# Down products of an unpacked MLP by seven products instead of eight, beside the next sequence's delta attention

## The chip, the core and the metric

The kernel runs on one core of a Trainium2 chip. The metric is the device time of one execution in microseconds, the median over several executions. Everything is in fp32. A matmul instruction of the program shows as two records in the profile, so counts of PE records are twice those of the program.

## The reference

Two sequences of 1024 tokens with 512 features go through two pre-norm layers, each an attention and an MLP, each added to a residual stream x:

```
x = x + delta_attention(layernorm(x))      # gated delta rule, 6 heads of 64, causal conv
x = x + mlp0(layernorm(x))                 # 512 -> 4096 -> 512, 4-bit weights with block scales
x = x + latent_attention(layernorm(x))     # 16 heads
x = x + mlp1(layernorm(x))                 # 512 -> 2048 -> 512, SiLU, hidden kept 2 of 4
# mlp0:
inter = gelu(x @ Wg.T) * (x @ Wu.T)
out = inter @ Wd.T
```

The 4-bit codes and scales of Wg, Wu and Wd are input. The change concerns the last line, for sequence 0.

## The kernel before, in words

The work is laid out in stages, each a pair of streams that share the engines: a "main" stream of attention steps, and a "fill" stream of MLP pieces. `weave` (L157) advances the main stream by one step, gets back the microseconds of fill that this step wants (`FILL`, 3.3, for the delta attention), and draws pieces from the fill until their own estimates (`STEP`, 3.4, for four matmuls of 512 columns, half of that for a seven's product) have used this credit up. What is left of the fill when the main stream has ended runs alone. The order that comes out is the order in which PE, DVE (VectorE), ACT (ScalarE) and POOL (GpSimd) execute: these four are scheduled by hand. The DMA issues on SP (SyncE) are ordered by the framework.

The stages, read from the trace: to about 460 us the delta attention of sequence 0 and both sequences' front ends; to about 1242 the delta attention of sequence 1 (`Delta.second`), beside MLP 0 of sequence 0 (`Unpacked`); to 1288 the rest of that MLP alone; to about 2193 the latent attention of sequence 0 beside MLP 0 of sequence 1 (`Second`); then the attention of sequence 1 beside the sparse MLP of sequence 0; at last the sparse MLP of sequence 1 (`Sevens`).

MLP 0 is cut into eight chunks of 512 hidden features. `Unpacked` expands the codes on the way: for each half of a chunk's gate, up and down weights, `Codes.values` (L917 ff.) makes two pieces of three DVE instructions (nib, L925 and L926, and a multiplication with the scales, L929), and the result is also stored to DRAM (`kept`) for sequence 1. `plan` queues these pieces as jobs, three for each part (the third forms the left sums of a gate or up part on POOL and stores it), and `core.spend(n)` executes n jobs between two pieces of MLP work. The first two chunks go by plain matmuls (`chunk`). From the third on (`rest`), gate and up go by a scheme that multiplies two 2 x 2 block matrices with seven block products instead of eight (`SEVEN`, L211):

```
    (1, 0, True, "11", "11"),
    (2, 1, True, "12", "21"),
    (6, 0, False, "S2", "T2"),
    (5, 1, True, "S1", "T1"),
    (7, 0, False, "S3", "T3"),
    (3, 1, False, "S4", "22"),
    (4, 0, False, "22", "T4"),
```

Each row names the product, which of two PSUM banks it goes to, whether it starts the bank afresh, and the left and right factor. S1 to S4 and T1 to T4 are sums of blocks (`left_sums` and `right_sums`, from L226). Products 1, 6 and 5 are copied from PSUM by ACT (`part`, L991); after 2, 7, 3 and 4 DVE adds the bank to the destination, and for 2, 7 and 3 a copied part is added one product later (`soon`, run by `step`). `macro` does a gate or up half of a chunk in seven pieces of four matmul records of 512 columns (z_ps, L1018).

The down product of `Unpacked` is plain: `outcome` (L1154 ff.) takes the eight tiles of 128 tokens, multiplies each by the chunk's down weights with four matmuls of 512 columns into one bank (o_ps, L201), adds it to the token tile x on DVE (L1161), and spends one job. In the last chunk each x tile is stored (parked) right after its addition. The down products of `Second` already go by sevens: `Seven.output` (L1056 ff.) is called for two passes over half of the tokens, q = 0 and 1, each with seven products of four matmuls of 256 columns (z_ps, L1064); left sums of h on DVE (L957), right sums of the weights on POOL (L239 to L242 when called with POOL), x additions on DVE (L1079) and, for the copied parts, on POOL (L1081).

`Delta.second` works on eight chunks of 128 tokens as three overlapping streams per slot: `early` (prepare, then solve, a triangular solve on DVE by rows, L603 and L604), `late` (invert, then advance, which updates the state S: R at L683 and L684, matmuls L689, L397, L703 and L720, Ud at L693, o at L698 and L726, S at L715) and `normed`. `fetch` loads what the front end had stored for a chunk: cv, the convolved values, and gw, the output gate.

At the handover `mlp[1].open()` loads the first gate weights of `Second` (z_left) and sums them on POOL, then the first product of `Second` can start; its first two chunks' gate and up weights are stored without sums and are loaded as four blocks.

Of the kernel before, what the change touches and what calls it, by code (L numbers as in the profile page):

```python
# [26 lines left out]
F32 = mybir.dt.float32  # L27
# [9 lines left out]
P = 128  # L37
# [25 lines left out]
class Pools:  # L63


    def __init__(self, tc):
        self.tc, self.open_ = tc, {}
# [14 lines left out]
class Core:  # L82
# [171 lines left out]
class Delta:  # L254
# [570 lines left out]
    def second(self, stored, away, fill):  # L825


        core, nc, a = self.core, self.core.nc, self.a
        self.open(1, 2)

        def fetch(c):
            d = self.d[c]
            d["cv"] = self.ring("cv", [P, 3 * NG, P], 2)
            nc.sync.dma_start(out=d["cv"], in_=self.away[c][0])
            d["gw"] = self.ring("gw", [P, NH, DH], 3)
            nc.sync.dma_start(out=d["gw"], in_=self.away[c][1])
# [36 lines left out]
        for slot in range(CH + 2):  # L873
            if slot + 1 < CH:
                fetch(slot + 1)
# [84 lines left out]
class Seven:  # L960
# [95 lines left out]
    def output(self, left, right, at, adder):  # L1056
# [17 lines left out]
        for p, ps in self.products(multiply):  # L1074
# [6 lines left out]
                    self.soon.append(lambda x=x, v=parts[{2: 1, 7: 5, 3: 6}[p]]: adder.tensor_add(x, x, v))  # L1081
            yield p

    def places(self, x, q):

        dm = DM // 2
        return [
            [x[:, 4 * m + 2 * q : 4 * m + 2 * q + 2, v * dm : (v + 1) * dm] for v in range(2)] for m in range(2)
        ]


class Unpacked(Seven):
# [3 lines left out]

    EARLY = 2

    def __init__(self, core, banks, codes, xT, kept, park):
        super().__init__(core, banks, AF.Gelu_apprx_tanh, core.nc.vector)  # L1100
        self.codes, self.xT, self.kept, self.park = codes, xT, kept, park
        self.wp = core.pools("f_h", side="right")
        self.nib = core.pools("f_nib", 2, side="right")
        self.plain = core.pools("f_w", 2, side="right")
        early = (("gate", 0), ("up", 0), ("gate", 1), ("up", 1), ("down", 0), ("down", 1))
        later = (("gate", 0), ("up", 0), ("down", 0), ("gate", 1), ("up", 1), ("down", 1))
        self.order = [(c, *part) for c in range(NC0) for part in (early if c < self.EARLY else later)]
        self.ws = {}
        self.staged = {u: codes.load(u) for u in self.order[:2]}

    def tile(self, u):

        c, w, half = u
        away = self.kept[u]
        if w == "down":
            t = self.wp.tile([P, 2, 512], F32, tag="w_down", bufs=3, name="w_down")
# [37 lines left out]
    def outcome(self, c, hs, tbs):  # L1154

        core, nc = self.core, self.core.nc
        wd = [self.ws[c, "down", half] for half in range(2)]
        for n in range(4 * tbs[0], 4 * tbs[-1] + 4):
            po = self.banks.one("o_ps")
            product(nc, po, [(h, wd[s // 2][:, s % 2, :]) for s, h in enumerate(hs(n))])  # L1160
            nc.vector.tensor_add(core.x[n], core.x[n], po)  # L1161
            if c + 1 == NC0:
                nc.sync.dma_start(out=self.park[n], in_=core.x[n])
            core.spend(3 - len(tbs))
            yield STEP

    def chunk(self, c, tb, swap=None):
# [19 lines left out]
        yield from self.outcome(  # L1187
            c, lambda n: [h[:, s, n % 4 * P : n % 4 * P + P] for s in range(4)], (tb,)
        )
        core.spend()  # L1190

    def first_tokens(self):
# [16 lines left out]
    def macro(self, c, half, w, g):  # L1209

        left = self.blocks(self.ws.pop((c, w, half)))
        for p in self.gate(left, g) if w == "gate" else self.up(left, g):
            self.step(p, 0)
            self.core.spend(1)
            yield STEP / 2
        self.core.spend()

    def rest(self):
        core = self.core
        parts = ("gate", 0), ("up", 0), ("gate", 1), ("up", 1), ("down", 0), ("down", 1)  # L1220
        self.plan(0, *parts)
        for c in range(self.EARLY):
            yield from self.chunk(c, 1, self.swap if c + 1 == self.EARLY else None)
        for c in range(self.EARLY, NC0):
            gs = [self.wp.tile([P, 2, 2, T // 2], F32, tag=f"h{half}", name="h0") for half in range(2)]
            for (half, w), ahead in zip(
                ((0, "gate"), (0, "up"), (1, "gate"), (1, "up")),
                (("down", 0), ("gate", 1), ("up", 1), ("down", 1)),
            ):
                self.plan(c, ahead)  # L1230
                yield from self.macro(c, half, w, gs[half])
            self.step(4, 0)
            self.plan(c + 1, ("gate", 0), ("up", 0))
            yield from self.outcome(
                c,
                lambda n: [gs[s // 2][:, s % 2, n // 4, n % 4 * P : n % 4 * P + P] for s in range(4)],
                (0, 1),
            )
            core.spend()
        core.pools.close("f_z", "f_nib", "f_h")  # L1240


class Second(Seven):
# [41 lines left out]
    def right_factors(self, wd):  # L1285
        half = DM // 2
        blocks = {
            f"{i + 1}{j + 1}": wd[:, 2 * i : 2 * i + 2, j * half : (j + 1) * half] for i in range(2) for j in range(2)
        }
        new = [self.wp.tile([P, 2, half], F32, name=f"wd_t{i}") for i in range(2, 5)]  # L1290
        right = right_sums(self.core.nc.gpsimd, blocks, new)
        return {name: [t[:, k, :] for k in range(2)] for name, t in right.items()}

    def left(self, hs, q, calls):

        blocks = {
            f"{i + 1}{j + 1}": hs[j][:, :, i, q * HB : (q + 1) * HB] for i in range(2) for j in range(2)
        }
        new = [self.wp.tile([P, 2, HB], F32, name=f"h_s{i}") for i in (1, 2, 4)]
        return left_sums(Recorder(self.core.nc.vector, calls), blocks, new)  # L1300

    def run(self):
        core, nc = self.core, self.core.nc
        todo, ws = self.todo, self.ws
        for c in range(NC0):
            wd = self.down_weights(c)
            hs = []
            for pair in range(2):
                g = self.wp.tile([P, 2, 2, T // 2], F32, tag=f"h{pair}", name="h0")
                hs.append(g)  # L1310
                for w in ("gate", "up"):
# [4 lines left out]
                    for p in self.gate(left, g) if w == "gate" else self.up(left, g):  # L1316
# [1 line left out]
                        if p == 3 and i < len(todo):  # L1318
                            self.sums(todo[i])
                        if p == 3 and (w, pair) == ("up", 0):  # L1320
                            right = self.right_factors(wd)
                        yield STEP / 2
            calls = deque()
            lefts = [self.left(hs, 0, calls)]
            for q in range(2):
                for p in self.output(lefts[q], right, self.places(self.x, q), nc.gpsimd):
                    self.step(p, 0)
# [2 lines left out]
                        while calls:  # L1330
                            calls.popleft()()
                    if q == 0 and p == 4:
                        lefts.append(self.left(hs, 1, calls))
# [661 lines left out]
def two_layers(ctx, tc, a):  # L1995
# [1 line left out]
    core = Core(ctx, tc)  # L1997
    pools = core.pools
    banks = Banks(ctx, tc)
    core.hold(pools("x0", side="right"), 0)  # L2000


    kept = {}
# [10 lines left out]
    mlp = []  # L2014

    def some():
        mlp.append(Unpacked(core, banks, Codes(core, pools("codes", 2, side="right"), a), xT_0, kept, parks[0]))
        return mlp[0].first_tokens()

    delta.first(xT_0, some)  # L2020
# [125 lines left out]
```

## Time and profile before

| | |
|---|---|
| median of 3 runs | 3213.23 us (3211.96 to 3216.2) |
| the profiled execution | 3214.91 us, its span 3213.2 |
| mean granted TensorE clock | 0.979 |
| PE, DVE, ACT, POOL busy | 97%, 60%, 29%, 24% |
| HBM | 70 GB/s over the span |
| chain that ended last | PE 81%, DVE 9%, POOL, issue, ACT and DMA 2% each |
| x<-x,o_ps on DVE (L1161) | 64 of 686 ns |
| x<-x,z_ps on DVE (L1079, `Second`) | 64 of 683 ns |
| x<-x,part on POOL (L1081, `Second`) | 48, mean 1460 ns |
| right sums of wd on POOL (L239 to L242) | 32, 1275 to 1490 ns |
| part<-z_ps on ACT (L991) | 288 of 586 ns |

A row of groups names line, engine, operation, output and inputs, shape and count, then busy time in us and the mean of one in ns, then the idle time of that engine just before these instructions and what ended it. PE is the busy engine almost everywhere, so a change matters by what it does to the time of PE's own instructions and to the gaps between them. PE's clock is granted by the chip; the profile states it as a share of full speed for any stretch.

### The profile page before, as it was taken

The numbers are of one execution on the slowest core, as the hardware profiler recorded it, in microseconds if no ns is written. First come the engines' busy times: TensorE is split into PE (matmuls) and PEld (weight loads), VectorE is DVE, ScalarE is ACT, GpSimd is POOL, SyncE is SP. The second block draws the span as 40 slices with busy tenths as digits, with TensorE's granted clock in tenths as the row PEclk, the third lists the DMA queues.
The fourth block names the chain that finished last, engine by engine and source line by source line (L and its number), as shares of the span: only waits on it lengthen the run. The fifth ranks groups of instructions, "written<-read, shape, count | busy, mean of one in ns | idle before, by whom it ended". The sixth has DMA issues, their size and how long they took to land.

```text
span 3213.2 us, 35654 instructions
## 1 busy us (share of the span) xinstructions
PE 3106.8 (97%) x13012; PEld 1626.1 (51%) x13012; DVE 1925.1 (60%) x3569; ACT 931.2 (29%) x1338; POOL 766.6 (24%) x822
## 2 busy tenths in 40 slices
PE   7999899999999999999999999999999999999998
PEld 6787754555555554555434444446433243224547
DVE  6888752466666554367577656745674367244766
ACT  5544311122222211311453125522113401432221
POOL 3323101122222211356321221222003600450000
PEclk9999899999999999999999999999999999999999
DMA  2111234132332224246112111142010010015211
GB/s 90 35 29 29 67 96 142 32 122 91 97 95 86 76 94 164 70 137 207 66 37 69 53 48 37 35 141 72 20 40 1 14 53 14 7 37 167 76 46 49
DMA packets 194638, 228.08 MB, mean 71 GB/s; under 512 B 53728, under 2 KB 148448, under 8 KB 194080
## 3 DMA queue, kind: packets, MB, share of 16 engines
q1 hardware_dynamic: 194464, 225.81, 22.2%
q8 instruction: 103, 1.69, 0.2%
q14 instruction: 71, 0.58, 0.1%
HBM read 153.11 MB, written 72.61 MB: 70 GB/s over the span
## 4 chain that ended last, share of the span: by engine, by line
PE 81%; DVE 9%; POOL 2%; issue 2%; ACT 2%; DMA 2%; SPq 1%; DVEq 0%; POOLq 0%; ACTq 0%
PE z_ps L1018 23%; PE o_ps L201 12%; PE z_ps L1064 8%; PE u_ps L201 5%; PE g_ps L201 5%; PE st_ps L1564 5%; PE s_ps L1506 4%; PE av_ps L1582 3%; PE proj_ps L201 2%; PE small_ps L630 1%; PE wide_ps L640 1%; DVE cv L469 1%; PE wide_ps L558 1%; DVE rd L1634 1%; PE den_ps L1603 1%
## 5 line engine op out<-in xcount | busy, mean ns | idle before, releaser
L991 ACT COPY part<-z_ps 128x512 f32<-128x512 f32 x288 | 168.7, 586 | 738.4 <-PE z_ps L1018 505.5
L1018 PE MATMUL z_ps<-xT,z_left 128*128 128x512 f32 x768 | 361.8, 601 | 3.1 <-DMA z_left<-in_w_gate 3.0
L1515 DVE TENSOR_REDUCE top<-s_ps 128x2 f32<-128x1024 f32 x256 | 301.0, 1217 | 80.4 <-PE s_ps L1506 80.3
L1574 ACT ACTIVATE es<-st_ps 128x1024 f32<-128x1024 f32 x256 | 248.3, 1021 | 175.9 <-PE st_ps L1564 171.0
L1018 PE MATMUL z_ps<-xt,z_left 128*128 128x512 f32 x576 | 274.3, 598 | 1.2 <-DVE z_h L1036 1.0
L1018 PEld LDWEIGHTS z_ps<-xT,z_left 128*128 128x128 f32 x768 | 142.0, 191 | 191.6 <-issue 164.0
L201 PE MATMUL o_ps<-w_down,h 128*128 128x512 f32 x512 | 229.6, 599 | 0.4 <-DVE part L1052 0.4
L1596 POOL TENSOR_TENSOR es<-es 128x512 f32<-128x512 f32 x128 | 159.3, 1276 | 148.7 <-ACT es L1574 78.0
L1018 PE MATMUL z_ps<-xT,w_left 128*128 128x512 f32 x384 | 181.5, 602 | 5.0 <-DVE part L1052 2.7
L1564 PE MATMUL st_ps<-q,kT 17*128 17x512 f32 x1024 | 178.3, 650 | 4.3 <-ACT es L1574 1.1
L1018 PEld LDWEIGHTS z_ps<-xt,z_left 128*128 128x128 f32 x576 | 106.2, 190 | 145.7 <-issue 123.3
L1052 DVE TENSOR_TENSOR part<-z_ps,part 128x512 f32<-128x512 f32 x108 | 74.4, 689 | 174.1 <-PE z_ps L1018 168.5
L1506 PE MATMUL s_ps<-kT,q 16*128 16x512 f32 x1024 | 156.6, 647 | 6.6 <-DVE top L1515 6.6
L201 PEld LDWEIGHTS o_ps<-w_down,h 128*128 128x128 f32 x512 | 95.2, 191 | 110.5 <-issue 106.3
L201 PE MATMUL proj_ps<-xT,wqkv 128*128 128x256 f32 x576 | 136.6, 392 | 12.2 <-ACT gw L427 12.2
L1582 PE MATMUL av_ps<-es,v 128*32 128x512 f32 x1024 | 138.9, 615 | 0.0
L1018 PE MATMUL z_ps<-xt,w_left 128*128 128x512 f32 x288 | 137.0, 598 | 0.7 <-DVE part L1052 0.7
L1053 POOL TENSOR_TENSOR h<-h,part 128x512 f32<-128x512 f32 x48 | 66.5, 1387 | 280.1 <-DVE part L1052 280.1
L1621 DVE TENSOR_TENSOR acc<-acc,es 128x1024 f32<-128x1024 f32 x96 | 131.7, 1419 | 0.0
L201 PEld LDWEIGHTS proj_ps<-xT,wqkv 128*128 128x128 f32 x576 | 109.3, 195 | 31.6 <-ACT gw L427 15.1
L1036 DVE TENSOR_TENSOR h<-z_ps,part 128x512 f32<-128x512 f32 x84 | 57.9, 690 | 102.4 <-PE z_ps L1018 89.3
L201 PE MATMUL o_ps<-sdown,h 128*128 128x512 f32 x256 | 117.1, 601 | 0.0
(311 smaller groups left out, 5164.9 us busy)
## 6 DMA issues: line engine op xcount, KB each, us to landing
sums<-factor SPq DMA_DIRECT2D x24, 512.0 KB, 3.3
kept_gate<-w_left SPq DMA_DIRECT2D x12, 896.0 KB, 3.7
kept_up<-w_left SPq DMA_DIRECT2D x12, 896.0 KB, 3.9
z_left<-kept_gate SPq DMA_DIRECT2D x12, 896.0 KB, 4.6
z_left<-kept_up SPq DMA_DIRECT2D x12, 896.0 KB, 4.6
kept_down<-w_down SPq DMA_DIRECT2D x16, 512.0 KB, 3.0
wd<-kept_down SPq DMA_DIRECT2D x16, 512.0 KB, 4.2
xl<-park SPq DMA_DIRECT2D x32, 256.0 KB, 2.7
```

Source lines behind the costliest of these rows:

```text
L201: nc.tensor.matmul(ps, lhsT, rhs, start=(i == 0), stop=(i == len(pairs) - 1))
L991: self.core.nc.scalar.copy(t, src)
L1018: self.core.nc.tensor.matmul(ps, left[l][:, k, :], self.right[r][:, k, :], start=(first and k == 0), stop=(k == 1), skip_group_check=True,)
L1052: nc.vector.tensor_add(v, ps, v)
L1064: nc.tensor.matmul(ps[:, i * dm : (i + 1) * dm], left[l][:, k, i * P : (i + 1) * P], right[r][k], start=(first and i == 0 and k == 0), sto ...
L1506: nc.tensor.matmul(tiles[h4 // 2][:, h4 % 2 * 512 : h4 % 2 * 512 + 512], q1s[t][r : r + HALF, gr, :], kT[r : r + HALF, gr, j * 512 : (j + ...
L1515: nc.vector.tensor_reduce(top[:, j, h : h + 2], tiles[e].rearrange("p (i k) -> p i k", i=2), AX.X, ALU.max, negate=True)
L1564: nc.tensor.matmul(tiles[h4 // 2][:, h4 % 2 * 512 : h4 % 2 * 512 + 512], kT[r : r + CR, gr, kt * P : (kt + 1) * P], q2[r : r + CR, gr, :], ...
L1574: nc.scalar.activation(t.rearrange("p i q -> p (i q)"), tiles[e], AF.Exp, scale=HALF**-0.5)
L1582: nc.tensor.matmul(av[gr][32 * h4 : 32 * h4 + 32, :], v[:, kt, 4 * gr + h4, :], es[u][h4 // 2][:, h4 % 2, :], start=(kt == 0), stop=(kt == ...
L1596: nc.gpsimd.tensor_add(t, t, es[u][h4 // 2][:, h4 % 2, :])
L1621: nc.vector.tensor_add(t, es[u - 1][e] if kt == 1 else t, es[u][e])
```

## The change

Chunks 2 to 7 of sequence 0's MLP 0 get their down products by sevens. `outcome` stays for chunks 0 and 1; `outputs` takes its place in `rest`. With it come these edits:

- x of sequence 0 is one tile of 128 x 8 x 512 instead of eight, so that a pass can add to two token tiles at once.
- The down weights of a chunk are one tile of 128 x 4 x 512 with one buffer, `wd`, instead of two tiles from a ring of three. Its second half is unpacked during the gate half 1, together with up half 1 (six jobs), and nothing is planned for up half 1.
- `right_factors` (POOL) is called after product 3 of up half 1. `left` queues the sums of h on DVE: three at product 1 of a pass, the fourth at product 6. S3 and S4 are written over blocks of h.
- A fill piece of the down product is 1.7 us of estimate instead of 3.4, with one job each.
- The eight stores to park come together after the last chunk's second pass.
- In `Delta.second`, cv has one buffer instead of two and is fetched after the first step of the chunk's predecessor's prepare; gw has two buffers instead of three and is fetched with x in `late`.

Instructions of the program, before and after: PE 6996 and 7140 (192 matmuls of 512 columns less, 336 of 256 more), DVE 3571 and 3619, ACT 1340 and 1376, POOL 827 and 887, SP 1416 both.

```diff
     def hold(self, pool, b):
-        for n in range(b * TT, (b + 1) * TT):
-            self.x[n] = pool.tile([P, DM], F32, tag=f"x{n}", name=f"x{n}")
+        x = pool.tile([P, TT, DM], F32, name="x")
+        for n in range(TT):
+            self.x[b * TT + n] = x[:, n, :]
+        return x
...
-            d["cv"] = self.ring("cv", [P, 3 * NG, P], 2)
+            d["cv"] = self.ring("cv", [P, 3 * NG, P], 1)
             nc.sync.dma_start(out=d["cv"], in_=self.away[c][0])
-            d["gw"] = self.ring("gw", [P, NH, DH], 3)
-            nc.sync.dma_start(out=d["gw"], in_=self.away[c][1])
...
         def early(c):
             if c < CH:
-                yield from self.prepare(c)
+                steps = self.prepare(c)
+                next(steps)
+                if c + 1 < CH:
+                    fetch(c + 1)
+                yield
+                yield from steps
...
                 nc.sync.dma_start(out=x, in_=a["x"][(CH + c) * P : (CH + c + 1) * P, :])
+                gw = self.d[c]["gw"] = self.ring("gw", [P, NH, DH], 2)
+                nc.sync.dma_start(out=gw, in_=self.away[c][1])
...
+    def left(self, hs, q, calls, pool, again=False):
+        blocks = {
+            f"{i + 1}{j + 1}": hs[j][:, :, i, q * HB : (q + 1) * HB] for i in range(2) for j in range(2)
+        }
+        names = (1, 2) if again else (1, 2, 4)
+        new = [pool.tile([P, 2, HB], F32, tag=f"h_s{i}", bufs=1, name=f"h_s{i}") for i in names]
+        if again:
+            new.append(blocks["12"])
+        return left_sums(Recorder(self.core.nc.vector, calls), blocks, new)
...
+            if half == 0:
+                self.wd = self.wp.tile([P, 4, 512], F32, tag="wd", name="wd")
+            t = self.wd[:, 2 * half : 2 * half + 2, :]
...
             self.step(p, 0)
             self.core.spend(1)
+            if p == 3 and (half, w) == (1, "up"):
+                self.factors = self.right_factors(self.wd, self.sevens)
             yield STEP / 2
...
+    def outputs(self, c, gs):
+        core, nc = self.core, self.core.nc
+        calls = deque()
+        left = self.left(gs, 0, calls, self.sevens, True)
+        for q in range(2):
+            for p in self.output(left, self.factors, self.places(self.x, q), nc.gpsimd):
+                self.step(p, 0)
+                if p == 1:
+                    while len(calls) > 1:
+                        calls.popleft()()
+                elif p == 6:
+                    calls.popleft()()
+                elif p == 4 and q == 0:
+                    left = self.left(gs, 1, calls, self.sevens, True)
+                core.spend(1)
+                yield STEP / 2
+        if c + 1 == NC0:
+            self.step(4, 0)
+            for n in range(TT):
+                nc.sync.dma_start(out=self.park[n], in_=core.x[n])
+        core.spend()
...
-                (("down", 0), ("gate", 1), ("up", 1), ("down", 1)),
+                ((("down", 0),), (("gate", 1),), (("up", 1), ("down", 1)), ()),
             ):
-                self.plan(c, ahead)
+                self.plan(c, *ahead)
                 yield from self.macro(c, half, w, gs[half])
-            self.step(4, 0)
             self.plan(c + 1, ("gate", 0), ("up", 0))
-            yield from self.outcome(
...
-            core.spend()
+            yield from self.outputs(c, gs)
```

More of the change, by code (lines that the diff above doesn't have):

```diff
@@ L873, in second @@
         for slot in range(CH + 2):
-            if slot + 1 < CH:
-                fetch(slot + 1)
             streams = [normed(slot - 2), late(slot - 1), early(slot)]
@@ L1082, in output, with right_factors @@
             yield p
+    def right_factors(self, wd, pool):
+        half = DM // 2
+        blocks = {
+            f"{i + 1}{j + 1}": wd[:, 2 * i : 2 * i + 2, j * half : (j + 1) * half] for i in range(2) for j in range(2)
+        }
+        new = [pool.tile([P, 2, half], F32, tag=f"wd_t{i}", bufs=1, name=f"wd_t{i}") for i in range(2, 5)]
+        right = right_sums(self.core.nc.gpsimd, blocks, new)
+        return {name: [t[:, k, :] for k in range(2)] for name, t in right.items()}
+    def left(self, hs, q, calls, pool, again=False):
+        blocks = {
+            f"{i + 1}{j + 1}": hs[j][:, :, i, q * HB : (q + 1) * HB] for i in range(2) for j in range(2)
+        }
+        names = (1, 2) if again else (1, 2, 4)
[3 more added lines that the diff above has]
+        return left_sums(Recorder(self.core.nc.vector, calls), blocks, new)
     def places(self, x, q):
@@ L1097, with __init__ @@
     EARLY = 2
-    def __init__(self, core, banks, codes, xT, kept, park):
+    def __init__(self, core, banks, codes, xT, x, kept, park):
         super().__init__(core, banks, AF.Gelu_apprx_tanh, core.nc.vector)
-        self.codes, self.xT, self.kept, self.park = codes, xT, kept, park
+        self.codes, self.xT, self.x, self.kept, self.park = codes, xT, x, kept, park
         self.wp = core.pools("f_h", side="right")
@@ L1114, in tile @@
         away = self.kept[u]
-        if w == "down":
-            t = self.wp.tile([P, 2, 512], F32, tag="w_down", bufs=3, name="w_down")
+        if w == "down" and c + 1 < self.EARLY:
+            t = self.plain.tile([P, 2, 512], F32, tag="w_down", name="w_down")
+        elif w == "down":
+            if half == 0:
+                self.wd = self.wp.tile([P, 4, 512], F32, tag="wd", name="wd")
+            t = self.wd[:, 2 * half : 2 * half + 2, :]
         elif c < self.EARLY:
@@ L1152, in plan, with outcome @@
                 self.core.jobs.extend([lambda p=pieces: next(p, None)] * 3)
-    def outcome(self, c, hs, tbs):
+    def outcome(self, c, h, tb):
         core, nc = self.core, self.core.nc
         wd = [self.ws[c, "down", half] for half in range(2)]
-        for n in range(4 * tbs[0], 4 * tbs[-1] + 4):
+        for n in range(4 * tb, 4 * tb + 4):
             po = self.banks.one("o_ps")
-            product(nc, po, [(h, wd[s // 2][:, s % 2, :]) for s, h in enumerate(hs(n))])
+            col = slice(n % 4 * P, n % 4 * P + P)
+            product(nc, po, [(h[:, s, col], wd[s // 2][:, s % 2, :]) for s in range(4)])
             nc.vector.tensor_add(core.x[n], core.x[n], po)
-            if c + 1 == NC0:
-                nc.sync.dma_start(out=self.park[n], in_=core.x[n])
-            core.spend(3 - len(tbs))
+            core.spend(2)
             yield STEP
@@ L1186, in chunk @@
             self.plan(c + 1, ("gate", 1), ("up", 1), ("down", 0), ("down", 1))
-        yield from self.outcome(
-            c, lambda n: [h[:, s, n % 4 * P : n % 4 * P + P] for s in range(4)], (tb,)
-        )
+        yield from self.outcome(c, h, tb)
         core.spend()
@@ L1227, in rest @@
                 ((0, "gate"), (0, "up"), (1, "gate"), (1, "up")),
-                (("down", 0), ("gate", 1), ("up", 1), ("down", 1)),
+                ((("down", 0),), (("gate", 1),), (("up", 1), ("down", 1)), ()),
             ):
-                self.plan(c, ahead)
+                self.plan(c, *ahead)
                 yield from self.macro(c, half, w, gs[half])
-            self.step(4, 0)
             self.plan(c + 1, ("gate", 0), ("up", 0))
[L1234 to L1238, printed above, removed]
-            core.spend()
+            yield from self.outputs(c, gs)
         core.pools.close("f_z", "f_nib", "f_h")
@@ L1283, in down_weights @@
         return wd
[L1285 to L1300, printed above, removed]
     def run(self):
@@ L1320, in run @@
                         if p == 3 and (w, pair) == ("up", 0):
-                            right = self.right_factors(wd)
+                            right = self.right_factors(wd, self.wp)
                         yield STEP / 2
             calls = deque()
-            lefts = [self.left(hs, 0, calls)]
+            lefts = [self.left(hs, 0, calls, self.wp)]
             for q in range(2):
@@ L1332, in run @@
                     if q == 0 and p == 4:
-                        lefts.append(self.left(hs, 1, calls))
+                        lefts.append(self.left(hs, 1, calls, self.wp))
                     if q == 1 and p == 1:
@@ L1999, in two_layers @@
     banks = Banks(ctx, tc)
-    core.hold(pools("x0", side="right"), 0)
+    x_0 = core.hold(pools("x0", side="right"), 0)
     kept = {}
@@ L2016, in some @@
     def some():
-        mlp.append(Unpacked(core, banks, Codes(core, pools("codes", 2, side="right"), a), xT_0, kept, parks[0]))
+        mlp.append(Unpacked(core, banks, Codes(core, pools("codes", 2, side="right"), a), xT_0, x_0, kept, parks[0]))
         return mlp[0].first_tokens()
```

## The prediction

> **What bounds the kernel now.** I read the page first, then the stages by windows, then the chain of waits at the end of the stage that changes, then PE's waits and the timeline.
>
> ```profile
> span 3213.2 us, 35654 instructions
> PE 3106.8 (97%) x13012; PEld 1626.1 (51%) x13012; DVE 1925.1 (60%) x3569; ACT 931.2 (29%) x1338; POOL 766.6 (24%) x822
> ...
> L201 PE MATMUL o_ps<-w_down,h 128*128 128x512 f32 x512 | 229.6, 599 | 0.4 <-DVE part L1052 0.4
> ```
>
> PE is busy for 97% of the span, and the products that the change replaces had to wait only 0.4 us in all. (A matmul of the program stands as two records.) By stage, with the columns PE, PEld, DVE, ACT, POOL busy, clock:
>
> ```profile
> 660.00:1221.00 561.00, 551.33 (x2299) 310.12 (x2298) 327.00 (x705) 123.78 (x201) 134.04 (x151) 0.99 0.30 92
> 1260.00:1290.00 30.00, 30.00 (x71) 13.28 (x70) 6.96 (x11) 0.16 (x1) 0.66 (x2) 1.00 0.29 101
> 1490.00:2115.00 625.00, 623.12 (x2731) 282.99 (x2731) 411.73 (x458) 244.12 (x305) 147.13 (x117) 0.99 0.17 57
> ```
>
> 660 to 1221 is sequence 1's delta attention beside this MLP: PE is idle for 9.7 us of 561, while DVE, at 58%, and POOL, at 24%, have room on average. 1260 to 1290 is MLP work alone. 1490 to 2115 is the next MLP, whose down products go by sevens already: DVE at 66%, yet PE idle for 2 us. The chain at the handover to that MLP:
>
> ```profile
> 1253.44 7.13 PE z_ps L1018 x16
> 1260.58 27.47 PE o_ps L201 x64
> 1288.04 10.30 PE z_ps L1018 x24
> ```
>
> The last chunk's down products take 27.47 us, and `Second`'s first product follows without a wait. A seventh product, late in the next stage, beside a busy DVE:
>
> ```profile
> 2179.75 1.89 PE L1064 MATMUL z_ps<-wd,h 128*128 128x256 f32 x8
> ...
> 2181.91 1.89 PE L1064 MATMUL z_ps<-wd,h 128*128 128x256 f32 x8
> 2183.64 1.89 PE L1064 MATMUL z_ps<-wd_t,h_s 128*128 128x256 f32 x8
> 2186.23 1.99 PE L1064 MATMUL z_ps<-wd,h_s 128*128 128x256 f32 x8 [0.26 <-DVE x L1079]
> ```
>
> Eight records of 256 columns start 1.73 us after the last eight (2181.91 to 2183.64): 0.215 us each, as x64 in 27.47 is 0.429 for 512. And one place where PE waits:
>
> ```profile
> 1191.24 1.16 PE L397 MATMUL wide_ps<-S,qkT 64*128 64x64 f32 x12
> 1193.73 2.56 PE L689 MATMUL small_ps<-R,X 128*128 128x64 f32 x12 [1.33 <-DVE R L684]
> 1196.22 2.03 PE L397 MATMUL wide_ps<-S,qkT 64*128 64x64 f32 x12
> 1198.18 4.99 PE L201 MATMUL o_ps<-w_down,h 128*128 128x512 f32 x8
> ```
>
> Twelve L397 take 1.16 us before the wait of 1.33 and 2.03 after it; eight L201 take 4.99, not 3.43. The granted clock is 0.66 from 1193 to 1203.
>
> **Products: -20.6 us.** A chunk's down product is 32 matmuls, 64 records, 27.47 us. By sevens it is 2 passes x 7 products x 4 matmuls = 112 records of 0.2145 = 24.0. 3.43 saved, times six chunks. The weave gives the delta steps 3.3 us of fill each as before, so the time comes off the end of the stage, where the MLP runs alone. There are 112 weight loads for 64, at 190 ns. The Trainium skill ("TensorE: Matmul & The Clock Gate", Back-to-back issue gap) says that the spacing of load-and-matmul pairs is set by both; if they added, a chunk would cost 112 x (0.190 + 0.2145) = 45 us, six of them +106. The 1.73 us above has just such pairs, and decides: loads are hidden.
>
> **Finer fill: -4.6.** The 1.33 us wait arises where a delta step gets no piece of fill, because a piece is 3.4 us against a credit of 3.3. In the changed order 1.7 us pieces stand there. The wait goes, and the 3.3 us that the slow clock costs (0.34 of 10 us). Next there is DVE's R chain itself, 1.2 us, under 1.7 of fill.
>
> **DVE in the first of a chunk's two passes: +13.4.** What is added is cheap on average: per chunk 8 sums of h at 0.69 and 8 x adds of 0.68 for 8 old ones of 0.69. But the four unpack pieces of the next chunk (0.42 + 0.43 + 0.69 = 1.54 each) now fall in the first four products, and a bank must be drained in one product of 1.72 us where it had 3.44. In 17.8 us of PE, DVE has adds 2.7, s1 to s4 2.7, unpack 6.2, the last up product 1.4, and its delta share of about 3.7, 6 or more where the solve rows fall there. The order on DVE is fixed, so I set the two orders side by side. Chunk 2: PE from the end of product 2 to product 4 has, from the same lines' rows, L689 about 1.4, L397 1.1, products 6 and 5 3.44, L703 1.1, L720 1.3, products 7 and 3 3.44: 11.8. DVE has to be through with what remains of s1 to s3 1.5, an unpack piece 1.54, add 0.68, unpack 1.54, Ud and o 1.1, solve rows 7 to 10 2.3, s4 0.69, unpack 1.54, S twice 1.42, o 0.56, rows 11 to 13 2.6, and only then product 7's add 0.68: 16.2. Product 4, which reuses the bank, is 4.4 late; three later lags bring about 7.0. Chunk 5, counted in the same way (s4 2.5 late, product 7's add 3.3, then 0.6): 6.4. Chunks 3, 4, 6 and 7 have no solve rows there: 0 to 0.5 each, 1.5 together. Bounds for all: 5 (if DVE enters these passes ahead) to 22.
>
> **Clock after these gaps: +4** (0 to 10). After 1.33 us of wait the clock fell; after 0.9 us (three waits near 822, 899 and 1253) it did not; after 3.68 us near 645 it was 0.58 for 8 us. The skill's clock gate part (same page, Part 1) has the clock fall only after an idle window of about 3.4 us. By that rule only one gap here is long enough; by the 1.33 us row each of about three costs 3.3. I take a little over one.
>
> **POOL and ACT: 0.** POOL gets 4 right sums at 1.27 and 6 x adds at 1.3 to 1.5 per chunk, 13 to 14 us on an engine that is idle for three quarters of the stage. The right sums are issued after product 3 of the last up quarter; product 6 is the first to need a late one, T2, the third (3.8 us), and three products (5.2) and delta steps stand before it. The delta chain over POOL (AT, the block inverse) has about 5 us. Uncovered, each would cost at most its 1.3 us. ACT's 6 copies of 0.586 replace nothing and add 3.5 us per chunk on an engine at 22%. A rule that speaks against the change is in "SBUF — State Buffer", Who interferes with whom: a DVE instruction with two SBUF inputs and a POOL instruction that reads SBUF lock each other out for an instruction's length. The h sums have a median of 0.69 and a maximum of 1.75, the nib operations 0.42 and 2.02, which fits. If each of 10 POOL operations per chunk delayed DVE by half its length, it would be 6.5 us of DVE per chunk; but the next stage has the same ten and PE idle for 2 us in 625, so I take nothing, and leave the lock to the slow rival.
>
> **Memory, one tile of x, cv and gw: 0.** SP has as many issues. `cv` with one buffer is fetched after prepare's first step, when its transposes are done, and needed a slot later; `gw` comes with `x`, more than 10 us ahead of its use. Bounds 0 and 3 if a fetch landed late once.
>
> **Handover: +7** (3 to 9). Before, the loads of z_left for `Second` were issued at 1249 and its kept_up at 1255, ahead of the parks; the parks were spread over eight L201 tiles. Now eight parks wait on the last adds, on DVE and then POOL, in one block, and stand on SP ahead of the z_left loads. SP issues in order, 0.33 us each. From the last product: POOL's add about 0.4 after, four parks behind it 1.3, and the load lands 2.7 later: 4.3 of PE idle. The page's median landing for z_left is 4.6, which gives 6. The clock: after a 3.02 us wait for z_left at 2906 it was 0.50 to 2910 and 0.89 to 2914, 2.3 us; after 3.68 us it cost 3.3. 4.3 + 2.7.
>
> **Sum.** -20.6 - 4.6 + 7.0 + 6.4 + 1.5 + 4 + 7 = +0.7 on the profiled execution's 3214.91 us (span 3213.2, 1.7 around it), which lies 1.7 over the median, 3213.23. So about 3214. 0.2%, what a measurement of this kernel can tell from no change, is 6.4 us.
>
> **The rivals.** *The gain arrives*: DVE keeps up, as it does in the next stage, where PE idles 0.26 us beside a saturated DVE. Against it: no unpack is in that stage. -20.6 - 4.6, handover +4 to +7, stalls 0 to 8, clock 0 to 3: 3192 to 3206, middle 3200. 0.31. *The gain is eaten*, as summed: 3207 to 3220. 0.35. *DVE's lateness takes over in every chunk* (the slower side): the first pass has 17.8 us of PE and about 16.7 of DVE in chunks 3, 4 and 6; from 1.1 us of lock-out by POOL per pass on, each gap passes 1.3 us and takes the clock along. Then three more gaps of 1.5 and 3.3, +14, and the full 3.3 in chunks 2 and 5, +2.6: 3231, 3220 to 3238. For it: the nib maximum of 2.02. Against it: the average loads. 0.34. *The change doesn't do what it says*: if loads paced the 256-column matmuls there would be no saving; the 1.73 us row excludes it.
>
> **How the numbers follow.** The eaten gain is the likeliest by a little, so its sum is the point, 3214; almost all of it lies within 0.2%. The gain case reaches from 3192 to 3206 with its middle at 3200, and about a third of its 0.31 lies under 3197; about a third of the slow case's 0.34 lies over 3230. That leaves out 0.1 on each side.
>
> **What would show it.** L1064-like products with starts 1.72 apart (first step); no PE wait for R near 1193 (second); PE waits for DVE's x adds in chunks 2 and 5, 4 and 3 us long, with PEclk dips behind (third, fourth); at the end a PE wait for the DMA into z_left of 4 to 6 us and slow first products (last). It is wrong if PE's waits for x adds stay under 3 us in all, if `Second` starts without a wait, or if the delta steps wait for POOL or for `cv`.

## The result and the profile after

The changed kernel took 3222.53 us (median of 8, 3216.96 to 3226.29) against 3212.3 (8 runs, 3206.05 to 3216.2): ratio 1.0033, interval 1.0022 to 1.0044. It is slower by 10 us. The profiled execution has a span of 3220.9 us. From its page, in the order of the lines shown of before:

```profile
span 3220.9 us, 36455 instructions
...
PE 3092.0 (96%) x13300; PEld 1683.7 (52%) x13300; DVE 1991.8 (62%) x3617; ACT 950.9 (30%) x1374; POOL 859.0 (27%) x882
```

PE has 15 us less to do, in a span that is 8 us longer. DVE has 67 us more, where 48 more instructions of 0.69 make 33. The same columns by window, 660 to 1221 as before, and the handover:

```profile
660.00:1221.00 561.00, 534.70 (x2496) 350.45 (x2494) 387.60 (x748) 140.54 (x231) 211.03 (x201) 0.99 0.31 95
...
1294.00:1300.00 6.00, 0.60 (x2) 0.43 (x2) 0.69 (x1) 0.00 (x0) 0.61 (x1) 0.82 0.73 236
1300.00:1308.00 8.00, 8.00 (x14) 3.28 (x14) 1.63 (x4) 1.03 (x2) 4.31 (x10) 0.71 0.89 279
```

PE's idle time in the first stretch goes from 9.7 to 26.3 us. PE's waits from 600 to 1300, the head of the list (total us, times, longest):

```profile
PE z_ps L1070 <- DVE x L1085: 8.1, 5, 3.8
PE z_ps L1024 <- DMA z_left<-kept_gate: 5.4, 1, 5.4
PE small_ps L705 <- DVE Ud L695: 4.6, 2, 3.7
PE z_ps L1070 <- DVE h L963: 3.8, 1, 3.8
...
PE small_ps L632 <- DMA T<-dT: 2.0, 2, 1.7
PE small_ps L151 <- DVE ln_xn L143: 1.1, 1, 1.1
```

The first, second and fourth are new, and so are the two at the end; Ud had 3.7 us in one wait before. The chain at the handover, which answers to the three lines shown of before (start, length, what):

```profile
1292.59 0.70 DVE x L1085
...
1293.35 1.27 POOL x L1087
...
1296.48 0.55 SPq L1320
...
1297.07 2.55 DMA z_left<-kept_gate
1299.62 10.47 PE z_ps L1024 x18
```

DVE's last add, POOL's add, the parks on SP, then the load: 7 us during which PE does nothing but end its last product.

Chunk 2's passes, PE first and then DVE at the same time:

```profile
738.22 0.94 PE L705 MATMUL small_ps<-Ud,kn 128*128 128x128 f32 x6 [0.94 <-DVE Ud L695]
738.99 1.45 PE L722 MATMUL small_ps<-U,pT 128*128 128x64 f32 x12
740.27 1.95 PE L1070 MATMUL z_ps<-wd_t,h 128*128 128x256 f32 x8
742.10 1.97 PE L1070 MATMUL z_ps<-wd,h 128*128 128x256 f32 x8
747.85 3.30 PE L1070 MATMUL z_ps<-wd_t,h 128*128 128x256 f32 x8 [3.78 <-DVE x L1085]
750.94 2.30 PE L1070 MATMUL z_ps<-wd,h 128*128 128x256 f32 x8
754.31 1.99 PE L1070 MATMUL z_ps<-wd,h 128*128 128x256 f32 x8 [1.07 <-DVE x L1085]
```

```profile
743.45 0.71 DVE L717 TENSOR_TENSOR S<-S,small_ps 64x192 f32<-64x192 f32 x2
744.19 0.56 DVE L728 TENSOR_TENSOR o<-o,small_ps 128x384 f32<-128x384 f32 x1
...
746.58 0.32 DVE L606 TENSOR_REDUCE inv<-prod 48x13 f32<-48x169 f32 x1
747.01 0.69 DVE L1085 TENSOR_TENSOR x<-x,z_ps 128x512 f32<-128x512 f32 x1
747.62 0.42 DVE L931 TENSOR_SCALAR nib<-codes 128x512 int32<-128x512 int32 x1
748.07 1.37 DVE L932 TENSOR_SCALAR nib<-nib 128x512 int32<-128x512 int32 x1
```

Product 7 (740.27) has long been done when DVE, after S, o and the solve rows, comes to its add at 747.01. The product that needs the bank starts 3.78 us late, as its record at 747.85 says, and takes 3.30 us instead of 1.95: the slow clock. A nib instruction beside POOL's add (747.84 to 749.15) takes 1.37 us, not 0.43.

For everything below I use the length of the stage, from the first z_ps<-w_left product to the first z_ps<-z_left product. The part before it has the same instructions in the same order on PE, DVE, ACT and POOL in these kernels, and still it ends between 642.5 and 654.4 us in their profiles, so whole spans of single profiles mislead by some 10 us. A stage is read from one profile too: plain_down below has the products of before and a stage 2.8 us shorter, so I make nothing of differences of 3 us between two stages. The stage of before and of after (columns as above):

```profile
642.50:1287.90 645.40, 629.60 (x2489) 346.54 (x2489) 375.20 (x798) 135.62 (x222) 150.63 (x175) 0.99 0.33 103
```

```profile
647.40:1299.60 652.20, 615.60 (x2776) 400.55 (x2776) 444.49 (x847) 156.11 (x258) 239.71 (x229) 0.99 0.32 100
```

The stage is 6.8 us longer: PE busy 14.0 less, PE idle 20.8 more (15.8 to 36.6).

### The profile page after: what moved, and what is told of

It is laid out like the page before. It is cut to its first block, busy times and chain, and to the rows that moved or that the text cites. A ratio compares the mean times of both kernels' runs of the same rounds, so it can differ in the third digit from the quotient of the medians.

```text
span 3220.9 us, 36455 instructions
## 1 busy us (share of the span) xinstructions
PE 3092.0 (96%) x13300; PEld 1683.7 (52%) x13300; DVE 1991.8 (62%) x3617; ACT 950.9 (30%) x1374; POOL 859.0 (27%) x882
## 4 chain that ended last, share of the span: by engine, by line
PE 79%; DVE 11%; POOL 3%; issue 2%; ACT 2%; DMA 1%; SPq 1%; DVEq 0%; POOLq 0%; ACTq 0%
PE z_ps L1024 24%; PE z_ps L1070 11%; PE o_ps L203 7%; PE u_ps L203 5%; PE g_ps L203 5%; PE st_ps L1596 5%; PE s_ps L1538 4%; PE av_ps L1614 3%; PE proj_ps L203 2%; DVE cv L471 1%; PE small_ps L632 1%; PE wide_ps L642 1%; DVE prod L605 1%; PE wide_ps L560 1%; PE den_ps L1635 1%
## 5 line engine op out<-in xcount | busy, mean ns | idle before, releaser
L997 ACT COPY part<-z_ps 128x512 f32<-128x512 f32 x324 | 189.5, 585 | 852.1 <-PE z_ps L1024 494.4
L1087 POOL TENSOR_TENSOR x<-x,part 128x512 f32<-128x512 f32 x84 | 117.9, 1405 | 277.7 <-DVE x L1085 263.9
L1070 PE MATMUL z_ps<-wd,h 128*128 128x256 f32 x544 | 130.1, 388 | 6.2 <-DVE h L963 3.8
L1085 DVE TENSOR_TENSOR x<-x,z_ps 128x512 f32<-128x512 f32 x112 | 75.9, 682 | 78.9 <-PE z_ps L1070 75.9
```

What stands on the lines that cost most here:

```text
L997: self.core.nc.scalar.copy(t, src)
L1070: nc.tensor.matmul(ps[:, i * dm : (i + 1) * dm], left[l][:, k, i * P : (i + 1) * P], right[r][k], start=(first and i == 0 and k == 0), sto ...
```

## The experiments

Ratios are against the kernel before, timed beside each. Stage, idle and busy are PE's in the stage of one profile, in us.

| kernel | ratio | interval | stage | idle | busy |
|---|---|---|---|---|---|
| before | 1 | | 645.4 | 15.8 | 629.6 |
| changed | 1.0033 | 1.0022 to 1.0044 | 652.2 | 36.6 | 615.6 |
| plain_down | 0.9997 | 0.9986 to 1.0007 | 642.6 | 13.4 | 629.2 |
| before_half_pieces | 0.9987 | 0.9976 to 0.9997 | 641.3 | 14.4 | 626.9 |
| z_early | 1.0024 | 1.0014 to 1.0034 | 646.9 | 29.2 | 617.7 |
| spread | 1.0027 | 1.0017 to 1.0036 | 649.0 | 34.2 | 614.8 |
| both | 1.0017 | 1.0009 to 1.0026 | 646.4 | 28.8 | 617.6 |
| all_loads | 0.9995 | 0.9987 to 1.0002 | 643.6 | 27.8 | 615.8 |
| no_pool_adds | 0.9999 | 0.9990 to 1.0009 | 643.2 | 29.9 | 613.3 |
| direct_adds | 1.0034 | 1.0021 to 1.0047 | 651.7 | 31.9 | 619.8 |
| no_h_sums | 0.9979 | 0.9970 to 0.9988 | 637.9 | 27.1 | 610.8 |
| moved_unpack | 0.9998 | 0.9989 to 1.0006 | 644.2 | 30.4 | 613.8 |
| sevens_3_6_7 | 0.9989 | 0.9978 to 0.9999 | 638.3 | 19.9 | 618.4 |
| sevens_3_4_6_7 | 1.0004 | 0.9992 to 1.0016 | 647.5 | 25.8 | 621.7 |

**plain_down**: memory and loads of the change, plain products.

```diff
-            yield from self.outputs(c, gs)
+            yield from self.flat(c, gs)   # outcome of before, on the one tile wd
```

> The changed kernel with its memory and loads (x of the sequence in one tile, wd with one buffer, cv with one and gw with two, fetched later, second half of the down weights unpacked earlier), but with the plain down products of before in 128x512 matmuls and parks tile by tile. Theory (the arrangement of memory and loads costs nothing): within 3 us of the kernel before, 3209 to 3216. Rival (cv or gw, fetched later, hold up PE at the starts of slots): 4 us or more above the kernel before.

0.9997. The arrangement of x, wd, cv and gw is free, as predicted; the stage is no longer than before.

**before_half_pieces**: the kernel before with finer fill.

```diff
-            product(nc, po, [(h, wd[s // 2][:, s % 2, :]) for s, h in enumerate(hs(n))])
+            for s, (l, r) in enumerate(pairs):
+                nc.tensor.matmul(po, l, r, start=s == 0, stop=s == 3)
+                if s == 1 and len(tbs) == 2:
+                    yield STEP / 2
...
-            yield STEP
+            yield STEP / len(tbs)
```

> The kernel before, with the plain down product of chunks 1 to 7 handed out in pieces of two matmuls (1.7 us) instead of four. Theory (part of the change's worth is its finer fill: no delta step without fill at 1193, the wait of 1.33 us and the slow clock behind it go): 3 to 5 us less than the kernel before. Rival (another delta step waits in its place): within 2 us.

0.9987, 4.2 us, with an interval that stays just under 1, and 4.1 in the stage. From 1185 to 1205 PE has no idle time and a clock of 1.00. This part of the change's worth can be had without the sevens.

**z_early**: z_left in a pool of its own, its first load ahead of the parks.

```diff
+    def ahead(self):
+        self.lp = self.core.pools("g_l")
+        self.todo = [(c, w, half) for c in range(NC0) for half in range(2) for w in ("gate", "up")]
+        self.ws = {self.todo[0]: self.weights(self.todo[0])}
...
             mlp.append(Second(core, banks, xT, x, kept, parks[0]))
+            mlp[1].ahead()
```

> The changed kernel, with the buffers for the next MLP's gate and up weights in a pool of their own that is opened earlier, so that the first weights are loaded ahead of the parks. Theory (the handover costs a wait for the load of z_left, 5.4 us, and the slow clock behind it, 2 to 3): 7 to 9 us less than the changed kernel, 3213 to 3216, no wait of PE for z_left near 1295. Rival (the load only moves, and the next thing, the left sums on POOL or the first x tile of the attention, is as late): less than 2 us gained.

1.0024, some 3 us less, which the two intervals do not separate: neither theory as it stood. The wait for z_left is gone, and the stage is 5.3 us shorter, but 14 us later there is another. DVE and then PE of this run:

```profile
1310.58 0.69 DVE L128 BATCH_NORM_STATS2 ln_st<-xl 128x6 f32<-128x512 f32 x1 [4.74 <-DMA xl<-park]
...
1311.61 1.29 DVE L1042 TENSOR_TENSOR h<-z_ps,part 128x512 f32<-128x512 f32 x2
```

```profile
1312.35 3.78 PE L1024 MATMUL z_ps<-xt,z_left 128*128 128x512 f32 x4 [3.70 <-DVE h L1042]
```

DVE stands for 4.74 us at the attention's second x tile, whose load is issued on SP behind wd, wlat, wqu, wkvu and rope; the MLP's adds are queued behind it, and PE waits 3.70. The changed kernel has no such wait, as PE was late there itself.

**all_loads**: z_early and spread, and the first wd load later.

```diff
-            wd = self.down_weights(c)
+            wd = self.down_weights(c) if c else None
...
+                        if p == 4 and wd is None:
+                            wd = self.down_weights(c)
```

> Early load of the next MLP's first weights and spread unpacking as before, and the load of its first down weights moved behind its first gate half, so that the attention's second x tile is loaded ahead of them. Theory (at the handover the wait for z_left was only replaced by DVE waiting for that x tile, 3.7 to 4.0 us of PE): no wait above 1 us from 1285 to 1320 but the one for POOL near 1340 that both kernels have, 4 to 6 us less than the run with both edits, about 3213 to 3215. Rival (x tiles are late for another reason, the memory that they reuse): the wait stays above 3 us.

0.9995, against 1.0017 for both: 0.22%, 7 us, and no wait of PE over 0.25 us from 1285 to 1330. The profiles show the 7 us where they should be: the fiftieth record of a z_left product starts 36.0 us after the first in both, and 29.3 after it here, as in before. In the changed kernel it is 32.0: 2.7 later, by the slow clock. With the wait of 5.40 the handover there costs 8.1 us.

**spread** and **both**: the unpack jobs spread over both passes; both adds z_early.

```diff
-                core.spend(1)
+                if (p in (2, 5, 3)) if q == 0 else (p in (1, 6, 7, 4)):
+                    core.spend(1)
```

> The changed kernel, with the six jobs that unpack the next chunk's first weights spread over all fourteen products of the two passes (every second one) instead of the first six. Theory (DVE is late in the first pass because four unpack pieces of 1.54 us lie among its adds): PE's waits for x adds and h sums in chunks 2 to 7, 16 us in the changed kernel's profile, fall to 4 to 8, and some slow clock goes with them: 8 to 14 us less, 3208 to 3214. Rival (it is the sums of h, the solve rows or a lock by POOL that make DVE late, not the unpacking): less than 4 us gained, and the waits in chunks 2 and 5 stay at about 5 us each.

> Both of the two edits together: early load of the next MLP's weights, and unpacking spread over both passes. Theory (two separate costs of a change that is a gain by itself): they add up, 16 to 22 us less than the changed kernel, 3200 to 3206, which is 0.2 to 0.4% under the kernel before. Rival (the gain of the products is lost at a third place too): not under 3209.

1.0027 and 1.0017: the rivals were right. Spreading takes 2 us off, within the intervals; the waits for DVE became 2.96 at product 4 of chunk 2 (3.78 before) and 1.63 and 2.56 in chunk 5 (3.83, 1.04, 1.01), with a new one of 2.41 for R at 755. Both together come to 5 us and stay 0.17% above the kernel before.

**no_pool_adds**: `self.soon = []` ahead of `self.step` in `outputs`, so that POOL's additions to x are left out.

> The changed kernel without POOL's 36 additions of copied parts to x (they are left out, so sequence 0's MLP 0 misses those terms). DVE's list of instructions is the same. Theory A (POOL's instructions lock DVE's two-input and nib instructions out, which is where the remaining waits come from): DVE's mean nib instruction (second one, 599 ns in the changed kernel, 463 with plain down products) and the h sums (863 to 1005 ns) come down most of the way, PE's waits in the stage fall by 6 us or more, 6 to 10 us less than the changed kernel, about 3213 to 3217. Theory B (DVE is late by the number and order of its own instructions): waits and time as in the changed kernel within 3 us.

0.9999, 11 us under the changed kernel: a little more than theory A had. The second nib instruction of DVE, from 640 to 1300 (count, busy us, mean ns), with plain down products, in the changed kernel, and here:

```profile
L932 DVE TENSOR_SCALAR nib<-nib 128x512 int32<-128x512 int32 x71 | 32.8, 463 | 2.4
```

```profile
L932 DVE TENSOR_SCALAR nib<-nib 128x512 int32<-128x512 int32 x72 | 43.1, 599 | 2.5
```

```profile
L932 DVE TENSOR_SCALAR nib<-nib 128x512 int32<-128x512 int32 x72 | 34.7, 481 | 2.5
```

So POOL's adds do stretch DVE's instructions, by 8.4 us over 72 of these, and the 48 sums of h by 5.4 (44.8 to 39.4). PE's idle time falls by 6.7 us, as theory A asked, but not mainly in the passes: the waits in chunks 2 and 5 are still 3.78 and 1.49, 2.90 and 1.32. The handover's wait is 2.72 us, not 5.40, without POOL's last add, and a wait of 2.14 for h, 13 us later, takes most of that back. PE's other waits in the stage fall by 4.0 us and its busy time by 2.3. A part of that is chance: after the same wait of 3.78 us the clock fell in the changed kernel and did not fall here (last section):

```profile
745.05 1.97 PE L1070 MATMUL z_ps<-wd_t,h 128*128 128x256 f32 x8 [3.78 <-DVE x L1085]
```

**direct_adds**: DVE adds those products from PSUM.

```diff
+            if p in (1, 6, 5) and adder is None:
+                x = {1: at[0][0], 6: at[0][1], 5: at[1][1]}[p]
+                nc.vector.tensor_add(x, x, ps.rearrange("p (i d) -> p i d", i=2))
```

> The changed kernel, in which DVE adds products 1, 6 and 5 from PSUM to x directly, in place of ACT's 36 copies and POOL's 36 additions: 36 instructions of 0.68 us more on DVE, none of them with two SBUF inputs. Theory A (lock by POOL): DVE's busy time in the stage rises by 24 for the adds and falls by 15 to 25 for the stretched ones, the time falls or stays, -5 to 0 us against the changed kernel. Theory B (count of DVE instructions): 8 to 20 us more than the changed kernel, 3230 to 3242.

1.0034, level with the changed kernel. DVE's busy time in the stage is 441.9 us against 444.5: 36 adds more (24.5 us), and all of it won back, most by the nib instructions (10.4) and the sums of h (9.3). POOL's help in these passes, with ACT's copies, costs DVE as much as the work itself.

**no_h_sums**: `left` returns plain blocks, nothing queued on DVE.

> The changed kernel without DVE's 48 sums of h (left out: the products take plain blocks of h in place of the sums, so sequence 0's MLP 0 is a wrong sum of products). POOL, ACT and PE have the same instructions. Theory B (DVE has too many instructions in these passes, the sums of h being the ones that the change adds): DVE's busy time in the stage falls by 35 to 45 us, PE's waits on DVE in chunks 2 and 5 fall from 4.9 and 5.9 to 1 to 3 each, 8 to 12 us less than the changed kernel. Theory C (the solve rows stand ahead of the x adds whatever else is there): waits of 3 us or more stay in both chunks, under 5 us gained.

0.9979, 17 us less: more than Theory B asked for, though its waits are not there. Chunk 2 has 2.41, 1.01 and 1.50, chunk 5 has 4.16. The waits of 3 us that Theory C wanted in both stay in one. What went is the handover's wait (h_s is not allocated, and z_left is loaded at 1261, with the eight parks as late as ever) and 5 us of PE's busy time. So the parks on SP are not what makes z_left late. It is the added tiles: without h_s, or in a pool of its own (z_early, 1273), z_left is loaded ahead of the parks. This run takes out the tiles and the sums that fill them together, and the traces hold no addresses, so that the tiles share memory with z_left is inferred.

**moved_unpack**: on all_loads, no unpacking in the first pass.

```diff
+                if (half, w) == (1, "up"):
+                    self.plan(c + 1, ("gate", 0))
                 yield from self.macro(c, half, w, gs[half])
-            self.plan(c + 1, ("gate", 0), ("up", 0))
+            self.plan(c + 1, ("up", 0))
...
-                core.spend(1)
+                if q and p in (6, 7, 4):
+                    core.spend(1)
```

> The run with all loads, and the unpacking of the next chunk's first weights taken out of the first pass altogether: the gate part is unpacked beside up half 1, which had no jobs, and the up part in the last products of the second pass. Theory B (what makes DVE late in chunks 2 and 5 is the sum of its work there; without any unpacking it has 11 to 12 us for 11.8 us of PE): no wait above 1 us for x adds or h sums in either pass, 7 to 12 us less than the run with all loads, 3200 to 3205 beside a kernel before of 3212, clearly faster than both kernels. Theory C (solve rows ahead of the adds): the waits of 3.0 and 2.6 us stay, under 3 us gained.

0.9998: the waits that theory B named are gone, 0.97 us in chunk 2 and 0.31 and 1.05 in chunk 5, and the time is no shorter than with all loads. Others took their place:

```profile
PE z_ps L1024 <- DVE part L1058: 7.2, 4, 2.4
PE small_ps L632 <- DMA T<-dT: 4.7, 2, 3.0
PE z_ps L1070 <- DVE x L1085: 4.0, 4, 1.1
```

The unpacking now lies among up's adds (part) and ahead of the solve, whose result reaches PE through memory (T). The waits were moved, not removed.

**sevens_3_6_7** and **sevens_3_4_6_7**: all_loads, sevens only in some chunks.

```diff
-            yield from self.outputs(c, gs)
+            yield from self.outputs(c, gs) if c in SOME else self.flat(c, gs)
```

> The run with all loads, with down products by sevens only in chunks 3, 6 and 7, whose passes do not meet the solve rows or the state update of a full slot; chunks 2, 4 and 5 go plainly in pieces of 1.7 us. Theory (a pass by sevens gains where DVE has no solve rows beside it): products -10.3, finer fill -4, of which 2 to 6 are lost to small waits: PE's waits in the stage about 18 to 21 us, 3200 to 3207 beside a kernel before of 3213, faster than both kernels. Rival (DVE's late work turns up as a wait wherever the passes are put, so waits stay at 27 us): 3209 or more.

> As the run with sevens in chunks 3, 6 and 7, with chunk 4 by sevens too; its second pass lies at the state update and the solve rows of a slot. Theory (place decides): the 3.4 us of the fourth chunk are lost again to waits there: same as the three chunks within 2 us, waits 3 to 5 us longer. Rival (every chunk by sevens gains its 3.4 us): 3 to 4 us less than with three chunks.

With three chunks 0.9989: PE idle 19.9 us as the theory had it, the stage 7.1 us shorter than before, but the median, 3209.68 beside 3214.64, is over the 3200 to 3207 given and where the rival put it. (The profile is of its slowest run, 3216.34.) With the fourth chunk 1.0004, 5 us more where at most 2 were expected: waits are up by 6 (1.43 and 1.87 in chunk 4's passes; 1.3 of the rest stands at chunk 7, 4.26 for 2.93), and the slow clock costs 8.9 us of the stage for 3.3. Place decides, by the waits; one comparison of 5 us, at intervals of some 3 to 4 either way, is all that stands behind the time. Three chunks are 0.44% under the changed kernel and 0.11% under the kernel before, which is no better than before_half_pieces alone.

## Why the prediction was right and wrong

The time lies in the range, 3197 to 3230, and over the point, 3214: forecast no change, measured 10 us slower. That the costs would eat the gain, and which ones, held. That they would stop at the gain did not: the gain was smaller than predicted, and some waits were put at nothing. By the prediction's own terms, from the two profiles:

| term | predicted | measured |
|---|---|---|
| products, at full clock | -20.6 | -15.4 |
| slow clock at 1193 | -3.3 | -3.4 |
| slow clock after the new gaps in the stage | +4 | +4.9 |
| slow clock at the handover, behind the end of the stage | +2.7 | +2.5 |
| wait for R at 1193 | -1.3 | -1.3 |
| DVE late in the passes (x 8.1 + 0.6, h 3.8, Ud 0.9) | +14.9 | +13.4 |
| PE idle at the handover | +4.3 | +5.4 |
| other waits (T by DMA 2.0, ln_xn 1.1) | 0 | +3.1 |
| sum | +0.7 | +9.2 |

Without the slow clock behind its end the stage has 6.7 of this, where its length says 6.8. The measured clock terms are half of the time that PE is busy under a granted clock of 0.50; the products are the rest of PE's busy time, which makes them an estimate.

*Products*: mis-sized, the largest miss. At full clock PE's work in the stage is 622.9 us before and 607.5 in the changed kernel; the eight other kernels with six chunks by sevens have 606.1 to 608.1. The down products' records, each counted to the start of the next, went from 167.3 us to 150.0. That is 0.436 each before and 0.223 after, where the prediction had 0.429 and 0.2145 from the end of the stage and from the next one. Beside the delta attention products are dearer: from 740.27 to 742.10 above, where a delta product stands before, it is 1.83 us and not 1.73, and with pieces half as long that is met more often. The remaining 1.9 us are in other records and not explained.

*Finer fill, -4.6*: right; before_half_pieces gives 4.2 by itself.

*DVE in the first pass*: right in place and size. Chunk 2 was to be 4.4 late at product 4 and 7.0 in all; it is 3.78 there and 5.8 with Ud and the next. The working counted the S additions as 1.42, but the row's 0.71 (743.45 above) is for both; with that put right it gives 3.7 at product 4. Chunk 5 was to be 6.4 late; it is 5.9. The cause was put too narrowly, though: four unpack pieces. Without them there the time does not fall (moved_unpack): DVE has 375 us of work in the stage before and 444 after, and where the pieces went instead, PE waited for other instructions.

*Clock, +4 and +2.7*: right in sum, by luck in the parts. I took a little over one slow stretch of 3.3 us ahead of the handover; there were three of half that cost: 0.83 from 748 to 758, 0.82 from 913 to 920, 0.83 from 1076 to 1086. At the handover the clock was 0.82 and 0.71. The fall at 913 follows a wait of 2.42 us outside a pass, which was not foreseen. The rule of the Trainium skill ("TensorE: Matmul & The Clock Gate", Part 1), a fall after an idle window of about 3.4 us, would have had none there; the row of 1.33 us as a threshold would have had one after the 1.51 us at 663 and the 1.75 us at 1100 too, where the clock stayed at 1.00. The same part of the skill calls this window free-running, which I left out of account; in that the traces agree (last section).

*POOL, 0*: wrong step. "The next stage has the same ten and PE idle for 2 us in 625, so I take nothing": the next stage has no nib instructions. DVE gained 69 us in the stage; 33 are the 48 sums of h at 0.69 each, the rest mostly stretching: the sums take 11.7 more than that, the nib instructions 14 more than before. The rule that I named, from the Trainium skill ("SBUF — State Buffer", Who interferes with whom), is for DVE instructions with two SBUF inputs, as the sums of h are, and their fall from 44.8 to 39.4 us without POOL's adds agrees with it. The nib instruction has one input; the same section says that a tensor_scalar, which it is, can run in a mode that contends with POOL too, and no trace here shows whether it did. How much of the time is POOL's doing stays open: without its adds 11 us go, but the waits in chunks 2 and 5 are still 5.3 and 4.2 us of 5.8 and 5.9; the waits for T and ln_xn were not separated.

*Memory, 0*: right for cv, gw, wd and x (plain_down), but wrong at the end of the stage. The handover was put down to the parks on SP; it is the new tiles, most likely their memory, that keep z_left from being loaded before them (no_h_sums). The size, 7, was near: it was 8. Behind it lay a second late load, the attention's x tile, which costs nothing until the first is mended (z_early).

The slow rival, DVE late in every chunk, is near in time but did not happen as told: chunks 3, 4 and 6 have no wait for an x add over 0.65 us. The rival in which the gain arrives needs DVE to keep up, and it came only in part, where three chunks avoid the solve rows.

Still open: the terms give 9 us, the medians 10. After the stage the changed kernel's profile is 4.0 us faster than before's in spite of the slow clock there, and ahead of it 4.9 slower, in unchanged work; profiles of single executions can't resolve it.

## What to carry to other kernels

A saving on the busiest engine is paid for by the engine that serves it. Count that engine's instructions where the order puts them, not on average: at 58% of the time busy, and 69% with the change, it was late at the dense places, and moving 6 us of its work from one of them brought new waits at others. Take the cost of a product from a stretch with the same neighbours. When a stage uses more memory to its end, look at which load of the next stage has lost its early start, and what is queued behind that one; try the fineness of the pieces by itself, since here it alone (0.13%) did as much as the best kernel with sevens (0.11%).

## What the hardware showed that was not expected

The length of a wait did not tell whether the clock would fall; where it lay did. In each of the fourteen profiles the slow stretches at 0.50 last 3.41 us or a multiple of it (the one that ends the profile is cut short), and their starts lie on one grid of 3.41 us, placed differently in every execution. In the changed kernel they start at 652.74, 748.31, 912.15, 1075.99 and 1297.86: 28, 48, 48 and 65 steps apart. Two waits of 3.78 us at the same place, in the changed kernel and in no_pool_adds, cut along their grids (behind the stretch its length, then PE's busy time; the clock is third from the end):

```profile
741.48:744.90 3.42, 2.58 (x12) 1.75 (x10) 3.25 (x8) 0.12 (x1) 0.00 (x0) 1.00 0.81 307
744.90:748.31 3.41, 0.47 (x2) 0.47 (x3) 3.10 (x9) 0.40 (x1) 0.47 (x1) 1.00 0.10 31
748.31:751.72 3.41, 3.41 (x9) 2.52 (x9) 3.34 (x5) 0.00 (x0) 2.19 (x3) 0.50 0.07 13
```

```profile
739.86:743.27 3.41, 1.41 (x7) 0.91 (x5) 3.17 (x9) 0.52 (x1) 0.00 (x0) 1.00 0.72 204
743.27:746.69 3.42, 1.64 (x8) 1.44 (x8) 3.17 (x8) 0.00 (x0) 0.13 (x1) 1.00 0.04 10
746.69:750.10 3.41, 2.32 (x10) 1.44 (x8) 3.27 (x8) 0.59 (x1) 3.33 (x5) 1.00 0.30 89
```

In the first, 2.94 us of idle time fall into one step, and the next is slow; in the second, 2.00 and 1.78 fall into two, and none is. Counted from 600 to 1290 us over all fourteen profiles, among steps at full clock: all 36 in which PE was idle for 2.02 us or more were followed by a slow one, 6 of the 36 with 1.33 to 2.00, and 1 of the 2690 with less. So, by chance, the same wait costs another 1.7 us or nothing.

POOL's additions from and to SBUF also made DVE's one-input nib instruction take 599 ns on the mean instead of 481, single ones 1.37 us; replaced by DVE's own additions from PSUM, DVE had no more busy time (441.9 us) than with POOL's help (444.5).
